# Scan products of a four-layer image kernel summed by TensorE transposes, tokens on partitions, in place of products with the identity

## The chip, the cores and the metric

The kernel runs on one core of a Trainium2 chip. The metric is device time in microseconds (us), the median of several runs. One core has five engines[...]: PE (TensorE, matrix products; its weight loads are listed apart as PEld), DVE (VectorE), ACT (ScalarE), POOL (GpSimd) and SP (SyncE, which here issues most DMA transfers).

## The reference, cut to what matters

Four layers run over four images of 384 channels and 48 x 48 points, each added to its own input. Layer 0, where the change lies, is a Mamba block over the 2,304 points of an image as a sequence (768 inner channels, 16 states):

```python
def step(h_prev, inp):
    x_t, dt_t, B_t, C_t = inp
    dA = jnp.exp(dt_t[..., None] * A)
    dBx = dt_t[..., None] * B_t[:, None, :] * x_t[..., None]
    h_new = dA * h_prev + dBx
    y_t = jnp.einsum('bds,bs->bd', h_new, C_t)
    return (h_new, y_t)
...
y = ys.transpose(1, 0, 2) + xin * D
y = y * jax.nn.silu(z)
out = y @ out_proj_w.T
```

So for each channel, 16 state sequences are scanned, each is multiplied with its C, the 16 products are summed, and D times the block's input is added (the skip). Then come a gate with silu(z), an output projection and a layer norm. Layers 1 to 3 (a block-wise Fourier filter with a gate, a depthwise 11 x 11 convolution, four experts chosen by token) do not change.

## The kernel before, in words

**Tiles and stages.** All data are float32. An image's sequence is cut into five chunks of 460 (the last 464) tokens. Channels lie on the 128 partitions and tokens along the free dimension, so 768 inner channels are six groups m, taken in three pairs p. A chunk has 96 units (`unit`, L615): for each pair, 16 states s with the two groups of the pair in turn. In a unit:

- SP loads bc, the rows B and C of state s repeated over all partitions (L622, once for two units);
- ACT makes da = exp(dt x A) in PSUM (L626; two buffers);
- POOL makes bu = u x B (L630; three buffers);
- DVE runs the scan (L634), into da, or for every third unit into g;
- the product with C goes into a tile g (six buffers): by DVE (L640), or for each third unit, whose scan wrote g itself, by POOL (L651);
- ACT copies the last scan value into `carry` for the next chunk (L642, L650);
- PE adds g into y, one PSUM bank for each group of the pair (tags y0 and y1, one buffer each), by a matrix product with the identity as stationary operand (`summed`, L590, the matmul at L600).

A product of POOL is put off: `late` holds it until two further units have issued their sums, and `after` keeps the two in that order on PE.

**Skip, gate and tail.** `skip` (L609) adds D x input in the middle of a pair, as a matmul with d_diag, a diagonal matrix made from D at the start (L296). `gate` (L655) multiplies y with silu(z) on DVE, straight from PSUM into zs. `tail` (L716) yields the output projection in four parts (`out_proj`, L661), the layer norm and three `residual` pieces, whose results are turned back to channels by transposes (L704).

**Order of the work.** `scans` (L414) runs over the 20 chunks. For each, `plan` lays pieces at unit numbers of the coming 96: projections of the next chunk (`project`, `project_z`, `expand`), `steps` (dt and u of a pair), gates and the tail of the chunk before. After each unit, `tile_layers` may also issue pieces of layers 1 to 3 of earlier images from a queue; the pace is by unit number. The queue starts with unit 24 of image 1 and is longer for images 2 and 3, which have experts too. From the pieces, the Tile scheduler makes the final order on each engine, so a piece may move by some places. After the last scan, the rest of layers 1 to 3 runs alone.

**PSUM.** A pool named mm has two banks for projections and other short results (tag mm), two for da and one each for y0 and y1; the background queue has its own.

## Time and profile before

| What | Value |
|---|---|
| median of 3 runs | 5762.97 us (5753.89 to 5764.69) |
| profiled execution: its own time | 5767.51 us |
| its span, first to last instruction | 5765.7 us |
| granted TensorE clock, mean | 0.953 |
| scan L634, one | 1.17 us |
| product on DVE L640 / on POOL L651, one | 0.63 / 1.16 us |
| da on ACT L626 / carry L642, one | 0.65 / 0.16 us |
| y matmuls L600 (g with ident) | 3,840, 0.60 us each as drawn |
| PE's idle time before y matmuls, ended by DVE's g L640 | 282 us |

Busy time is that in which an engine had an instruction in flight. Successive matmuls overlap in the pipeline, so the length drawn for one is more than it takes in a row of them; the distance from start to start shows that. The profiled execution lies 4.5 us over the median. The span is 1.8 us under its execution's own time.

### The profile page before, as it was taken

How to read it: one execution, taken by the hardware profiler on the slowest of the kernel's cores; microseconds unless marked ns; L12 is line 12 of the kernel's file. 1: busy time of each engine (PE TensorE's matmuls, PEld its weight loads, DVE VectorE, ACT ScalarE, POOL GpSimd, SP SyncE). 2: the span in 40 equal slices, each digit the busy share in tenths (PEclk: the TensorE clock that was granted, in tenths of full speed). 3: DMA queues.
4: the chain of work that ended last, by engine and by line, in shares of the span. 5: the costliest groups of instructions: out<-in, count | busy, mean ns of one | idle time of the engine just before them, and what ended most of it. 6: DMA issues, size and time to landing. Idle time of an engine off the chain costs nothing. (4 is left out here: it accounts for less than half of the span.)

```text
span 5765.7 us, 69035 instructions
## 1 busy us (share of the span) xinstructions
PE 5255.3 (91%) x23236; PEld 3320.9 (58%) x23236; DVE 4030.3 (70%) x5653; ACT 2956.1 (51%) x6424; POOL 3110.3 (54%) x2795
## 2 busy tenths in 40 slices
PE   6888888988889999999887999999988799999999
PEld 3333333433455546777433664877634375789999
DVE  5988988899997796666899577656698856451110
ACT  3555555555566654444655565444455564335321
POOL 3877888766586685555565366545465646000000
PEclk9999989988999999999998899999989899899999
DMA  4444444434344363233333235323332323311100
GB/s 135 134 137 135 143 127 139 124 118 121 118 139 137 114 206 108 89 106 112 112 119 106 90 120 171 99 88 102 103 112 95 121 93 125 114 45 43 54 23 26
DMA packets 396011, 634.19 MB, mean 110 GB/s; under 512 B 32373, under 2 KB 386789, under 8 KB 392190
## 3 DMA queue, kind: packets, MB, share of 16 engines
q1 hardware_dynamic: 382148, 618.58, 33.7%
q10 hardware_dynamic: 13498, 11.11, 0.7%
q8 instruction: 184, 3.01, 0.2%
q14 instruction: 181, 1.48, 0.1%
HBM read 571.80 MB, written 57.80 MB: 109 GB/s over the span
## 5 line engine op out<-in xcount | busy, mean ns | idle before, releaser
L630 POOL TENSOR_TENSOR bu<-u,bc 128x460 f32<-128x460 f32 (+1 forms) x1920 | 2217.2, 1167 | 1346.3 <-DVE g L634 632.8
L600 PE MATMUL y<-g,ident 128*128 128x460 f32 (+1 forms) x3840 | 1838.3, 597 | 286.8 <-DVE g L640 282.2
L626 ACT ACTIVATE da<-dt,a_neg 128x460 f32<-128x460 f32 (+1 forms) x1920 | 1232.1, 646 | 268.5 <-DVE g L640 166.2
L634 DVE TENSOR_TENSOR_SCAN da<-da,carry,bu 128x460 f32<-128x460 f32 (+1 forms) x1008 | 1165.7, 1170 | 196.6 <-ACT da L626 170.1
L600 PEld LDWEIGHTS y<-g,ident 128*128 128x128 f32 x3840 | 704.3, 201 | 1008.1 <-DVE g L640 541.7
L651 POOL TENSOR_TENSOR g<-g,bc 128x460 f32<-128x460 f32 (+1 forms) x660 | 766.7, 1162 | 249.4 <-DVE g L634 128.0
L640 DVE TENSOR_TENSOR g<-da,bc 128x460 f32<-128x460 f32 (+1 forms) x1260 | 775.9, 627 | 109.7 <-PE y L600 80.1
L634 DVE TENSOR_TENSOR_SCAN g<-da,carry,bu 128x460 f32<-128x460 f32 (+1 forms) x528 | 617.2, 1169 | 134.1 <-PE y L600 67.9
L1139 PEld LDWEIGHTS ph<-xe,w 128*128 128x128 f32 x4608 | 596.7, 191 | 54.3 <-issue 40.4
L1157 PEld LDWEIGHTS pout<-hr,w 128*128 128x128 f32 x4608 | 591.4, 190 | 54.7 <-issue 43.8
L1139 PE MATMUL ph<-xe,w 128*128 128x144 f32 x4608 | 620.1, 288 | 0.0
L1157 PE MATMUL pout<-hr,w 128*128 128x144 f32 x4608 | 616.4, 287 | 1.5 <-DVE xe L1168 1.5
L642 ACT COPY carry<-da 128x1 f32<-128x1 f32 x1008 | 158.0, 157 | 884.2 <-DVE g L640 882.5
L998 PEld LDWEIGHTS pc<-band,row 128*128 128x128 f32 x3456 | 455.8, 194 | 81.1 <-issue 48.6
L1147 ACT ACTIVATE hr<-ph,nb 128x144 f32<-128x144 f32 x768 | 235.5, 377 | 507.3 <-PE ph L1139 506.9
L998 PE MATMUL pc<-band,row 128*128 128x162 f32 (+14 forms) x3456 | 469.2, 286 | 6.5 <-ACT row L987 4.7
L669 PE MATMUL po<-w_out,zs 128*115 128x384 f32 (+1 forms) x960 | 346.6, 494 | 11.1 <-DVE zs L659 7.7
L878 DVE SCALAR_TENSOR_TENSOR dw<-pad,w_dw,dw 128x384 f32<-128x384 f32 x576 | 342.2, 609 | 14.4 <-ACT pad L866 11.2
L634 DVE TENSOR_TENSOR_SCAN da<-da,nil,bu 128x460 f32<-128x460 f32 x252 | 291.5, 1170 | 74.3 <-ACT da L626 66.4
L490 PE MATMUL pin<-xch,w_inx 128*128 128x463 f32 (+2 forms) x720 | 323.1, 579 | 10.8 <-DVE dt L585 4.7
L518 PE MATMUL pinz<-xch,w_inz 128*128 128x460 f32 (+1 forms) x720 | 306.0, 559 | 12.0 <-DVE xc L507 7.9
L507 DVE SCALAR_TENSOR_TENSOR xc<-pin,conv_w,xc 128x460 f32<-128x460 f32 (+1 forms) x360 | 246.9, 686 | 76.6 <-ACT xc L502 73.9
(170 smaller groups left out, 4754.8 us busy)
## 6 DMA issues: line engine op xcount, KB each, us to landing
bc<-bcd SPq DMA_DIRECT2D x768, 460.0 KB, 3.6
bc<-bcd SPq DMA_DIRECT2D x192, 464.0 KB, 3.6
xs<-x1d SPq DMA_DIRECT2D x24, 576.0 KB, 4.3
x2d<-xs SPq DMA_DIRECT2D x24, 576.0 KB, 2.9
x<-x2d SPq DMA_DIRECT2D x12, 1152.0 KB, 6.5
x3d<-x SPq DMA_DIRECT2D x12, 1152.0 KB, 5.9
xg<-x3d SPq DMA_DIRECT2D x24, 576.0 KB, 4.6
xe<-x3d SPq DMA_DIRECT2D x64, 216.0 KB, 2.6
```

The source lines that it names most:

```text
L490: nc.tensor.matmul(ps[:, lo : halo + n], lhsT=w_inx[:, k, bass.ts(j, P)], rhs=c["x"][:, k, lo : halo + n], start=k == 0, stop=k == CT - 1,)
L600: return nc.tensor.matmul(c["y", m][:, :n], lhsT=lhsT, rhs=src, start=c["terms", m] == 1, stop=c["terms", m] == DS + 1, skip_group_check=True,
L626: nc.scalar.activation(da[:, :n], c["dt", p][:, m % 2, :n], AF.Exp, scale=a_neg[:, m, s : s + 1])
L630: nc.gpsimd.tensor_mul(bu[:, :n], c["u", p][:, m % 2, :n], bc[:, 0, :n])
L634: nc.vector.tensor_tensor_scan(here[:, :n], da[:, :n], bu[:, :n], last if t else nil[:, 0:1], ALU.mult, ALU.add,)
L640: nc.vector.tensor_mul(g[:, :n], here[:, :n], bc[:, 1, :n])
L651: nc.gpsimd.tensor_mul(g[:, :n], here[:, :n], bc[:, 1, :n])
L669: nc.tensor.matmul(ps[:w, :C], lhsT=c["zs"][:, m, bass.ts(k, w)], rhs=w_out0[:, m, :], start=m == 0, stop=m == MT - 1,)
L878: nc.vector.scalar_tensor_tensor(v, src, w_dw[:, ct, k : k + 1], v, ALU.mult, ALU.add)
L998: nc.tensor.matmul(d["acc2"][:, : BANDS[k] * W].rearrange("p (h w) -> p h w", w=W)[:, lo - edges[k] : hi - edges[k], xlo:xhi], lhsT=d["row ...
L1139: nc.tensor.matmul(ps[:, bass.ts(m, EB)], lhsT=d["w1"][:, e, k, bass.ts(m, P)], rhs=d["x", s][:, k, :], start=k == 0, stop=k == CT - 1,)
L1157: nc.tensor.matmul(d["o"][:, bass.ts(m, EB)], lhsT=d["w2"][:, e, k, bass.ts(m, P)], rhs=d["h", s, e][:, k, :], start=e == 0 and m == 0 and ...
```

## The change

The sum of the 16 products and the skip is now made in another layout, with tokens on partitions. `turned` transposes a tile of [128 channels, n tokens] in four quarters of w = n/4 tokens (115 or 116), each into its own 128 columns of one bank; the four quarters accumulate over the units. D x input is made by ACT into a tile dx (from the buffers of g) and transposed as the first term at the start of the pair. When a pair has ended, `collect` copies both banks to SBUF tiles yt, and `gate` turns them back by four transposes into a bank of tag mm before DVE's multiplication. Gates stand three and six units into the next pair (or head the tail, at units 2 and 4 of the next chunk), the tail's other pieces one unit later or more. POOL's product is still added behind the sums of two later units, and on the side of DVE the copy of the carry still follows the product.

```diff
-        d_diag = wp.tile([P, MT, P], F32, name="d_diag")
-        for m in range(MT):
-            nc.scalar.activation(d_diag[:, m, :], ident, AF.Copy, scale=d_col[:, m : m + 1])
...
-            def summed(i, m, lhsT, src):
+            def turned(y, src, n, start, stop):
+                w = n // TT
+                return [
+                    nc.tensor.matmul(
+                        y[:w, bass.ts(k, P)],
+                        lhsT=src[:, bass.ts(k, w)],
+                        rhs=ident,
+                        is_transpose=True,
+                        start=start and k == 0,
+                        stop=stop,
+                        skip_group_check=True,
+                    )
+                    for k in range(TT)
+                ]
...
             def skip(i, p):
-                for m in (2 * p, 2 * p + 1):
-                    summed(i, m, d_diag[:, m, :], c["xc"][:, m, : CHUNKS[t]])
+                for h in range(2):
+                    m = 2 * p + h
+                    y = c["y", m] = mm.tile(
+                        [P, 512], F32, name=f"y{b}_{t}_{m}", tag=f"y{h}", bufs=1
+                    )
+                    dx = wk.tile([P, TM], F32, name=f"dx{b}_{t}_{m}", tag="g", bufs=6)
+                    nc.scalar.activation(
+                        dx[:, :n], c["xc"][:, m, :n], AF.Copy, scale=d_col[:, m : m + 1]
+                    )
+                    turned(y, dx, n, True, False)
...
-                    ins = summed(i, m, ident, g[:, :n])
-                    c["since"] = c.get("since", 0) + 1
-                    if late and (c["since"] >= 2 or (m % 2 and s == DS - 1)):
-                        after(late.pop(0)(), ins)
+                    ins = turned(c["y", m], g, n, False, s == DS - 1)
+                    c["since"] += 1
+                    if late and (c["since"] == 2 or (m % 2 and s == DS - 1)):
+                        for one in late.pop()():
+                            after(one, ins[-1])
...
+            def collect(i, p):
+                w = CHUNKS[t] // TT
+                for h in range(2):
+                    m = 2 * p + h
+                    yt = c["yt", m] = wk.tile([P, 512], F32, name=f"yt{b}_{t}_{m}", tag="yt")
+                    nc.scalar.copy(yt[:w, :], c["y", m][:w, :])

             def gate(i, m):
+                w = n // TT
+                ps = bank(f"pyb{b}_{t}_{m}")
+                for k in range(TT):
+                    nc.tensor.transpose(
+                        ps[:, bass.ts(k, w)], c["yt", m][:w, bass.ts(k, P)], ident[:w, :w]
+                    )
                 zm = c["zs"][:, m, :n]
-                nc.vector.tensor_tensor(zm, c["y", m][:, :n], zm, ALU.mult)
+                nc.vector.tensor_tensor(zm, ps[:, :n], zm, ALU.mult)
...
             def tail(i):
+                yield lambda: gate(i, MT - 2)
+                yield lambda: gate(i, MT - 1)
...
                 if i:
-                    for m in (MT - 2, MT - 1):
-                        plan(0, lambda m=m: gate(i - 1, m))
                     for k, piece in enumerate(tail(i - 1)):
-                        plan(3 + 2 * k, piece)
+                        plan(2 + 2 * k, piece)
...
-                            plan(2 * DS * p, lambda m=2 * p - 2 + h: gate(i, m))
+                            plan(2 * DS * p + 3 + 3 * h, lambda m=2 * p - 2 + h: gate(i, m))
...
-                    plan(2 * DS * p + DS, lambda p=p: skip(i, p))
                 for p in range(MT // 2):
+                    skip(i, p)
                     for q in range(2 * DS):
                         unit(i, 2 * p + q % 2, q // 2)
                         ...
+                    collect(i, p)
```

More of the change, by code (lines that the diff above doesn't have):

```diff
@@ L588, in steps, with skip @@
                     nc.gpsimd.tensor_mul(u[:, h, :n], dt[:, h, :n], c["xc"][:, 2 * p + h, :n])
-            def summed(i, m, lhsT, src):
+            def turned(y, src, n, start, stop):
[12 more added lines that the diff above has]
+                ]
+            def skip(i, p):
                 (b, t), c = G[i], st[i]
                 n = CHUNKS[t]
-                if ("y", m) not in c:
-                    c["y", m] = mm.tile(
-                        [P, 512], F32, name=f"y{b}_{t}_{m}", tag=f"y{m % 2}", bufs=1
-                    )
-                    c["terms", m] = 0
-                c["terms", m] += 1
-                return nc.tensor.matmul(
-                    c["y", m][:, :n],
-                    lhsT=lhsT,
-                    rhs=src,
-                    start=c["terms", m] == 1,
-                    stop=c["terms", m] == DS + 1,
-                    skip_group_check=True,
-                )
-            def skip(i, p):
-                (b, t), c = G[i], st[i]
-                for m in (2 * p, 2 * p + 1):
-                    summed(i, m, d_diag[:, m, :], c["xc"][:, m, : CHUNKS[t]])
+                for h in range(2):
+                    m = 2 * p + h
+                    y = c["y", m] = mm.tile(
+                        [P, 512], F32, name=f"y{b}_{t}_{m}", tag=f"y{h}", bufs=1
+                    )
+                    dx = wk.tile([P, TM], F32, name=f"dx{b}_{t}_{m}", tag="g", bufs=6)
[3 more added lines that the diff above has]
+                    turned(y, dx, n, True, False)
             def unit(i, m, s):
@@ L651, in unit @@
                     nc.gpsimd.tensor_mul(g[:, :n], here[:, :n], bc[:, 1, :n])
-                    late.append(lambda: summed(i, m, ident, g[:, :n]))
+                    late.append(lambda: turned(c["y", m], g, n, False, s == DS - 1))
                     c["since"] = 0
+            def collect(i, p):
+                (b, t), c = G[i], st[i]
+                w = CHUNKS[t] // TT
[3 more added lines that the diff above has]
+                    nc.scalar.copy(yt[:w, :], c["y", m][:w, :])
             def gate(i, m):
@@ L775, in scans @@
                         yield b, t, 2 * DS * p + q
+                    collect(i, p)
                 assert not todo
-            for m in (MT - 2, MT - 1):
-                gate(len(G) - 1, m)
             for piece in tail(len(G) - 1):
```

## The prediction

> **What bounds the kernel now.** I read the page first, for its shares of busy time.

> ```profile
> PE 5255.3 (91%) x23236; PEld 3320.9 (58%) x23236; DVE 4030.3 (70%) x5653; ACT 2956.1 (51%) x6424; POOL 3110.3 (54%) x2795
> ...
> PE   6888888988889999999887999999988799999999
> ...
> DVE  5988988899997796666899577656698856451110
> ...
> PEclk9999989988999999999998899999989899899999
> ```

> PE and DVE take turns: where one row is high, the other is often lower. So I cut the span at the chunks. Each of the 20 chunks (image b, chunk t; written b.t) has 96 scans, and every 96th scan start gives 96, 1026 (1.0), 1709 (1.3), 2126 (2.0), 2683 (2.2), 3239 (2.4), 3507 (3.0), 4076 (3.2), 4620 (3.4) and 4863 us (end of the scans). Busy time by stretch: columns are stretch, length, then PE, PEld, DVE, ACT, POOL, granted clock, DMA.

> ```profile
> 96.00:1026.00 930.00, 768.60 (x1814) 329.40 (x1813) 827.78 (x1030) 503.45 (x1065) 769.00 (x685) 0.94 0.42 135
> ...
> 2126.00:2683.00 557.00, 554.40 (x2970) 408.74 (x2969) 358.15 (x468) 268.07 (x659) 312.02 (x276) 0.98 0.37 114
> 2683.00:3239.00 556.00, 473.38 (x1440) 237.18 (x1439) 459.34 (x678) 297.19 (x621) 312.54 (x285) 0.90 0.36 112
> 3239.00:3507.00 268.00, 261.87 (x1366) 181.60 (x1365) 186.96 (x246) 169.98 (x322) 155.82 (x138) 0.99 0.34 114
> 3507.00:4076.00 569.00, 565.84 (x3011) 411.78 (x3010) 356.26 (x464) 271.05 (x663) 311.08 (x275) 0.99 0.36 110
> ...
> 4620.00:4863.00 243.00, 236.07 (x1294) 168.41 (x1292) 174.54 (x223) 158.72 (x307) 153.15 (x135) 0.99 0.35 116
> ```

> In image 0 DVE is busy 828 of 930 us (89%). In 2.0, 2.1, 2.4, 3.0, 3.1 and 3.4 it is busy only 63 to 72%, and PE is always in work. A busy PE need not be a full one, so I take start-to-start times from the timeline of PE (start, length, group; the length runs to the modelled end of the last one).

> ```profile
> 311.41 0.56 PE L704 MATMUL pt<-ident,on 115*128 115x115 f32 x4
> 311.81 0.95 PE L600 MATMUL y<-g,ident 128*128 128x460 f32 x2
> 312.59 1.71 PE L600 MATMUL y<-xc,d_diag 128*128 128x460 f32 x4
> 314.14 0.94 PE L600 MATMUL y<-g,ident 128*128 128x460 f32 x2
> ```

> Each start follows the last by 0.385 us for 460 columns ((314.14-312.59)/4) and by 0.10 us for a transpose of 115 columns ((311.81-311.41)/4): both 0.84 ns a column. The two differ in count: y has 3,840 matmuls for 1,920 units, two for each float32 product, while the transposes of L704 number 240 = 20 chunks x 3 x 4, one each. Pricing every matmul of the trace at 0.84 ns a column, or 0.11 us if that is more, fills 99% of 2.1 and 3.1, 92 to 94% of 2.0, 2.4, 3.0 and 3.4, and about 71% of image 0. Waits in 2.0 and 2.1 agree that DVE is starved from PE's side there:

> ```profile
> DVE da L634 <- ACT da L626: 72.9, 70, 4.8
> ACT hr L1147 <- PE ph L1139: 47.9, 35, 10.6
> ...
> DVE g L634 <- PE y L600: 34.5, 21, 6.6
> DVE g L640 <- PE y L600: 26.2, 17, 4.1
> ```

> ACT stands in its queue behind a PE result, and its late da holds up the scan; or g's six buffers are full because PE has not read them.

> [...] (columns: length, PE busy, clock):

> ```profile
> 302.24:305.65 3.41, 0.95 (x3) 1.00 0.00 0
> 305.65:309.07 3.42, 3.32 (x5) 0.50 0.28 90
> ```

> Three transposes in one window, half clock in the next, and the y products then 0.77 us apart instead of 0.385. Setting the column time of each window against the next clock, I find the border at about 0.38 of a window (a matmul with few input rows, such as L574 with 25, counts in proportion). Whether transposes count, the trace cannot say: no window has more than 0.11 of them, and none falls between the two readings. [...]

> **The change, part by part.**
> (a) A unit's sum: two matmuls of 460 columns, 0.77 us, become four transposes whose moving operand is ident, 128 columns: 4 x 128 x 0.84 = 0.43 us. Saved 0.34 us of PE. Weight loads pass from ident to slices of g, but L600's loads already waited for DVE in the trace, and a 128-column load sustains 0.11 us a matmul (L979: 0.108), so loads bind by at most 4 x 0.11 = 0.44. That accumulating transposes keep this rate no trace shows; bounds: 0.10 (115 columns) to 0.14 us each (a whole weight load of L704, not overlapped), so 0.40 to 0.56 a unit. I take 0.43.
> (b) skip: likewise 0.34 us saved 120 times. With (a), 102 x 0.34 = 35 us a chunk.
> (c) gate: 24 new transposes a chunk at 0.10 = 2.4 us of PE. Net 32 us a chunk, 650 us of PE work in all.
> (d) ACT gains six dx (0.65 us, as da of L626) and six copies of y (0.70 us, as L707, 460 columns): 8 us a chunk on an engine at 51 to 74%. Hidden under DVE or PE, except at (f). Six d_diag activations of 0.39 us go from the set-up, in DMA waits: nothing.
> (e) DVE's gate reads PSUM as before (0.63 us), 3 and 6 units later; behind it only out_proj waits, now from the sixth unit on. zs is rewritten from unit 15, after out_proj's last at 12 instead of 9: cover shrinks from six units to three, some 6 us. Nothing. SP's loads shift by a few places, no DMA is added.
> (f) At each end of a pair, ACT's copies of y wait for the last Pool product, and da of later units stands behind them. By the built order, from the end of the 31st scan: Pool one bu (1.17) then that product (1.17), 2.4; four transposes and their latency (0.26), 3.2; two copies, 4.6; carry and da, 5.5. DVE has before it a scan, product, scan, scan, product: 3 x 1.17 + 2 x 0.63 = 4.8. So da is late by about 0.8 us, three times a chunk. In the 14 chunks not bound by PE: 34 us. Bounds: 0 if the scheduler's slack covers it, 1.7 us each (72 us) at half clock.
> (g) Clock. With y at 0.43 us a unit of some 1.95 us, a window without other matmuls has 0.22 of work and goes cold even if transposes count. Re-pricing y in each window of the trace: cold windows of image 0 rise from 13 to 40%, of image 1 from 8 to 20%; of 2.1 and 3.1 stay at 1%. At half clock a unit's transposes take 0.86 us, still under the period, so little is late: 15 us (0 to 40).

> Sum. In the six PE-bound chunks PE gives up 32 us each, and DVE, at 174 to 187 us of busy time plus its usual 10% idle, has room to take most: 27 us x 6 = 162. In 1.3 and 1.4, PE at 0.9 and DVE at 0.83 to 0.86: 10 each, 20. Against this (f) 34 and (g) 15. Net 133 us off the profiled 5767.5 (span 5765.7 and 1.8 around it): 5634. That execution is 4.5 us over the median shown, so I say 5630. The stretch after 4863 us (903 us) has no y work and stays.

> **The rivals.**
> 1. Transposes do not count for the clock. Re-priced so, 67% of windows in image 0 and 57% in image 1 go cold, 23% in 2.0 and 3.0, 36% in 2.4 and 3.4. PE's load, its work over its clock, is then about today's 0.71 and 0.82 in images 0 and 1 (0.51/0.67 = 0.76, 0.61/0.71 = 0.85), and the gain shrinks: 15 us x 4 + 27 x 2 = 114, less 34 for (f) and 52 for cold projections that ACT and DVE wait for: 28. About 5735. [...] Against: bursts of three projections take 2.3 us and rewarm the clock.
> 2. Slower: the same, and PE becomes the bound in the thin chunks. Other matmuls of image 1 need 92 to 108 us a chunk, y and gate 46. Around 146 us of work in 222 us a chunk, PE fills at a mean clock of 0.66; that is the point. A saturated cold PE has 0.5 x 100/146 = 0.34 of counted work, under the border, so it can stay cold. At clock 0.55 image 1 takes 5 x (146/0.55 - 220) = 225 us more, 2.2 and 3.2 some 20 each: minus 114 plus 34 plus 265, about 5950; nearer the point, 5800. Central 5850.
> 3. The ACT wait of (f) takes the whole place of the removed work, at 2 to 3 us for 60 pair ends: 5765, no change.
> 4. Nothing of (f) and (g) shows, and DVE fills the PE-bound chunks entirely: 5560.

> **How the numbers follow.** Forecast 0.52, own range 5560 to 5690; rival 1 0.20 (5680 to 5790); 2 0.15 (5775 to 6000); 3 0.08; 4 0.05. The range 5560 to 5800 leaves out most of rival 2, half of 4 and the edges. A change within 0.2% can hardly be told from none here (the three runs spread by 0.19%). Faster: nearly all of the forecast and 4, two thirds of 1: 0.71. Same 0.06. Slower 0.23.

> **What would show it.** (a) L591, four starts 0.107 us apart in warm stretches. PE-bound gain: the scan starts of 2.1 and 3.1 about 270 us apart, not 299; image 0 within 2% of 930. (f) ACT's yt waits for PE near 1 us each. (g) the granted clock of image 0 near 0.8; if it is under 0.7, rival 1, and if image 1 is under 0.66 with PE full, rival 2. I am wrong if accumulating transposes run slower than 0.14 us each.

## The result, and the profile after

The changed kernel takes 5794.45 us (median of 4 runs, 5790.45 to 5797.41) against 5762.28 for the kernel before beside it: a ratio of 1.0058, interval 1.0041 to 1.0075. It is slower by 0.6%, where 5630 and "faster" were forecast. Its profiled execution took 5794.86 us, its span is 5793.0.

PE was relieved: it has 315 us less busy time, although it has 4,560 more matmuls. (The forecast's 650 us is priced at full clock and from start to start, so it is no forecast of busy time.) The page's first two parts, answering those of before:

```profile
PE 4940.3 (85%) x27796; PEld 3836.1 (66%) x27796; DVE 4034.3 (70%) x5653; ACT 3060.4 (53%) x6658; POOL 3111.3 (54%) x2795
...
PE   6677777778788888999877898999977798999999
...
DVE  5888888889988887667798668666788767451110
PEclk9677677888889988999878799899978789899999
```

PE's row is lower in most slices with scans, DVE's is no higher on the whole, and the clock of the first fifth, nearly all 9 before, is now mostly 6 and 7. Stretches cut at scan starts (columns: stretch, length, PE, PEld, DVE, ACT, POOL, clock, DMA) are image 0, then 2.0 with 2.1, 2.2 with 2.3, 2.4, 3.0 with 3.1, and 3.4:

```profile
95.00:1066.00 971.00, 716.14 (x2918) 501.34 (x2916) 835.25 (x1030) 531.27 (x1123) 769.63 (x685) 0.75 0.41 129
2201.00:2729.00 528.00, 505.66 (x3425) 440.88 (x3424) 353.04 (x466) 275.88 (x681) 312.27 (x276) 0.95 0.38 118
2729.00:3321.00 592.00, 468.48 (x2122) 319.68 (x2121) 468.43 (x691) 324.33 (x683) 312.47 (x285) 0.81 0.32 104
3321.00:3561.00 240.00, 216.82 (x1368) 170.93 (x1368) 182.34 (x238) 160.58 (x298) 155.63 (x138) 0.94 0.40 132
3561.00:4096.00 535.00, 514.01 (x3463) 443.13 (x3462) 348.68 (x458) 277.22 (x684) 311.63 (x276) 0.96 0.37 117
...
4664.00:4891.00 227.00, 204.89 (x1319) 171.09 (x1318) 168.82 (x216) 145.68 (x275) 150.03 (x133) 0.89 0.38 123
```

The two PE-bound stretches fell from 557 and 569 to 528 and 535 us. Image 0 rose from 930 to 971. 2.4 fell by 28, but 2.2 with 2.3 rose by 36. The next table, in us, cuts the whole difference at scan starts. Of the forecast, the 34 us of (f) are spread over its 14 chunks, and the 15 us of (g) stand in the row of image 0:

| stretch | before | after | difference | forecast |
|---|---|---|---|---|
| 2.0, 2.1, 3.0, 3.1 | 1125.2 | 1063.4 | -62 | -108 |
| 2.2 to 2.4, 3.2 to 3.4 | 1611.9 | 1626.8 | +15 | -44 |
| 1.3, 1.4 | 416.7 | 419.2 | +3 | -15 |
| image 0 and 1.0 to 1.2 | 1612.9 | 1687.4 | +75 | +34 |
| after the scans | 902.8 | 901.7 | -1 | 0 |

The price of a transpose was right. On the timeline of PE (start, length, group), first at half clock (0.50 granted from 601.5 to 609.5 us), last at full clock (1.00 from 2465 to 2467):

```profile
602.78 2.05 PE L591 MATMUL y<-ident,g 128*115 128x128 f32 x8 [0.62 <-DVE g L643]
606.53 2.91 PE L591 MATMUL y<-ident,g 128*115 128x128 f32 x12 [1.70 <-DVE g L643]
...
2465.74 1.04 PE L591 MATMUL y<-ident,g 128*115 128x128 f32 x8
```

At half clock, four more take 0.86 us more: 0.215 each. At full clock, starts are 0.109 us apart (median of all in the trace), where 0.107 was priced. What DVE and ACT wait for tells where the gain went (waits: total us, times, longest):

```profile
DVE da L637 <- ACT da L629: 331.3, 241, 13.2
...
ACT zs L522 <- PE pinz L515: 124.0, 68, 7.2
...
PEld y L591 <- ACT yt L665: 88.9, 34, 9.6
...
ACT dt L578 <- PE pdt L571: 65.9, 51, 3.8
```

In the kernel before, the first read 236.5, the second 83.1, the last 23.5, and the third did not exist. DVE's waits on y fell (those of its scans and products into g, together, from 170 to 95 us), but its waits on ACT's da rose by 95: in all, DVE's idle time in the part with scans is 998 us, before 973. So DVE waits for ACT where it had waited for PE. That alone doesn't make ACT the cost: in e10_skip_back (below), 86 us faster than the kernel before, DVE's wait on da still stands at 276.5.

At a pair end the wait for ACT can be read step by step (timeline, ACT and then DVE, at the end of the second pair of 0.2):

```profile
609.32 1.23 ACT L613 ACTIVATE dx<-xc,d_col 128x460 f32<-128x460 f32 x2
...
612.56 1.07 ACT L665 COPY yt<-y 115x512 f32<-115x512 f32 x2 [1.27 <-PE y L591]
613.51 0.20 ACT L654 COPY carry<-g 128x1 f32<-128x1 f32 x1
...
614.37 1.18 DVE L637 TENSOR_TENSOR_SCAN da<-da,carry,bu 128x460 f32<-128x460 f32 x1 [1.07 <-ACT carry L645]
```

A scan into g ended at 611.5; elsewhere in this stretch its carry and the next da follow at once, as at 608.64 and 608.74. Here they stand behind the two copies of y, which wait for PE's last transposes, and DVE, done with its product at 613.30, idles 1.07 us. Over the 60 pairs, DVE's idle time ahead of the first six scans of a pair, added up from the trace, rose from 193 to 245 us: 0.87 a pair. In the 14 chunks for which step (f) was meant it rose from 92 to 141, 49 us for the forecast's 34. Whether the copies are the cause of that is taken up below.

### The profile page after: what moved, and what is told of

It reads as the page before. It is cut to its first block, busy times and chain, and to the rows that moved or that the text cites. A ratio compares the mean times of both kernels' runs of the same rounds, so it can differ in the third digit from the quotient of the medians.

```text
span 5793.0 us, 78434 instructions
## 1 busy us (share of the span) xinstructions
PE 4940.3 (85%) x27796; PEld 3836.1 (66%) x27796; DVE 4034.3 (70%) x5653; ACT 3060.4 (53%) x6658; POOL 3111.3 (54%) x2795
## 5 line engine op out<-in xcount | busy, mean ns | idle before, releaser
L591 PE MATMUL y<-ident,g 128*115 128x128 f32 (+1 forms) x7680 | 1305.2, 318 | 403.0 <-DVE g L643 401.2
L591 PEld LDWEIGHTS y<-ident,g 128*115 128x115 f32 (+1 forms) x7680 | 1117.2, 202 | 700.1 <-DVE g L643 566.0
L1015 PE MATMUL pc<-band,row 128*128 128x162 f32 (+14 forms) x3456 | 493.6, 293 | 10.2 <-DVE x L1033 8.3
L1015 PEld LDWEIGHTS pc<-band,row 128*128 128x128 f32 x3456 | 466.7, 202 | 30.5 <-DVE x L1033 12.0
L515 PE MATMUL pinz<-xch,w_inz 128*128 128x460 f32 (+1 forms) x720 | 327.0, 588 | 33.9 <-DVE xch L730 12.6
L654 ACT COPY carry<-g 128x1 f32<-128x1 f32 x528 | 100.9, 191 | 392.8 <-DVE g L637 392.0
```

Source lines behind the costliest of these rows:

```text
L591: nc.tensor.matmul(y[:w, bass.ts(k, P)], lhsT=src[:, bass.ts(k, w)], rhs=ident, is_transpose=True, start=start and k == 0, stop=stop, skip ...
L1015: nc.tensor.matmul(d["acc2"][:, : BANDS[k] * W].rearrange("p (h w) -> p h w", w=W)[:, lo - edges[k] : hi - edges[k], xlo:xhi], lhsT=d["row ...
```

## Experiments

In the labels' numbers, 1 to 3 tell the clock from the order of the work, 4 and 8 undo the later tail, 5 to 7 put one side edit alone into the kernel before, and 9 to 12 follow from these. Ratios are to the kernel before on the same chip; differences between two of these kernels are taken from medians, and where the ratios say otherwise, that is said.

**e1_fill_thin: the clock given back.** Four more transposes, of a tile of zeros, go into y ahead of each unit's own in images 0 and 1 and in 2.2, 2.3, 3.2 and 3.3; the sums stay what they are.

```diff
+                        nc.tensor.matmul(
+                            y[:w, bass.ts(k, P)], lhsT=zero[:, :w], rhs=ident,
+                            is_transpose=True, start=False, stop=False,
...
+                    fill(i, c["y", m], n)
                     ins = turned(c["y", m], g, n, False, s == DS - 1)
```

> The changed kernel, with four more transposes a unit, of a tile of zeros, added into y in the chunks where PE has room (all of images 0 and 1; 2.2, 2.3, 3.2, 3.3). They change no sum; they only give TensorE work, 0.43 us a unit. Theory A (the half clock in windows with too little work costs the time, through projections that ACT waits for): the clock of image 0 rises from 0.75 to 0.93 or more, image 0 falls from 970 us to about 930, the 14 chunks give back most of the 136 us that they lost, total near 5660 us. Rival B (ACT's copies of y and dx, and what stands behind them, cost the time): image 0 stays near 970 us, total 5790 us or more.

5882.19 us, 1.0188 (1.0168 to 1.0207). Image 0 by stretches:

```profile
95.00:1076.00 981.00, 809.11 (x4823) 621.20 (x4821) 833.42 (x1031) 533.13 (x1124) 771.51 (x686) 0.94 0.41 128
```

With the clock back at 0.94, as before the change, image 0 is no shorter (980.5 against 971.9), and 2.2 and 2.3, back at 0.94 and 0.90, stay at 275 and 316 us. Giving the clock back doesn't shorten these stretches. But the filling itself costs PE time (65 of the 88 us by which this run is over the change lie in 1.3 and 1.4, where PE has other work), so this run alone doesn't price the clock. It shows one thing more: with nothing but transposes added, the clock of image 0 reads 0.94 in place of 0.75.

**e2_old_sum: everything but the transposes.** y is again a sum of products with ident, channels on partitions; D x by ACT, the copies of y and all places of gates and tail stay as in the change. The gate reads the copy, so the gate's transposes fall away.

```diff
                     nc.tensor.matmul(
-                        y[:w, bass.ts(k, P)],
-                        lhsT=src[:, bass.ts(k, w)],
-                        rhs=ident,
-                        is_transpose=True,
+                        y[:, :n],
+                        lhsT=ident,
+                        rhs=src[:, :n],
...
-                nc.vector.tensor_tensor(zm, ps[:, :n], zm, ALU.mult)
+                nc.vector.tensor_tensor(zm, c["yt", m][:, :n], zm, ALU.mult)
```

> The changed kernel with the old sum: y by products with ident, channels on partitions; dx, the copies of y by ACT, the places of gate and skip as in the change; the gate's transposes left out (DVE reads the copy). Theory A: the clock of image 0 is back at 0.93 or more, image 0 at 930 to 945 us, the six PE-bound chunks as slow as before, total 5765 to 5785 us. Rival B: the thin chunks are as slow as in the changed kernel and the PE-bound ones as slow as before, total near 5890 us.

5847.99 us, 1.0137 (1.0117 to 1.0157). Image 0:

```profile
95.00:1063.00 968.00, 789.20 (x1817) 336.40 (x1815) 846.27 (x1033) 530.97 (x1124) 775.00 (x686) 0.91 0.41 129
```

Without any transposed sum, at a clock of 0.91, image 0 takes 968 us, as in the change. So a loss of this size needs neither the transposes nor a low clock. But the run also brings in a cost that the change doesn't have: its gate reads both operands from SBUF, where that of the change reads one from PSUM. The gates of the change, then those of this run (count, shortest/median/longest in ns):

```profile
L677 DVE TENSOR_TENSOR zs<-pyb,zs x120: 610/628/644, 166.3 to 4899.3; 128x460 f32<-128x460 f32 x96, 128x464 f32<-128x464 f32 x24
...
L668 DVE TENSOR_TENSOR zs<-yt,zs x120: 610/642/1617, 164.5 to 4953.2; 128x460 f32<-128x460 f32 x96, 128x464 f32<-128x464 f32 x24
```

In this run 58 gates start while POOL is inside an instruction. Of these, 55 take 0.74 to 1.62 us and end 0.49 to 0.50 us after that instruction of POOL; none of the other 62 takes over 0.65. In the change 70 gates start so, and none is long. In all, the gates take 110 us here and 75 in the change. So of the 79 us lost here (0.0137 x 5770), up to 34 belong to this reading, and the 46 us (0.0079 x 5770) by which the change is faster than this run are not all the gain of its transposes.

**e3_both: both ways.** The new way only in chunks 0, 1 and 4 of images 2 and 3, the old one elsewhere.

```diff
+            def new(i):
+                b, t = G[i]
+                return b >= 2 and t in (0, 1, 4)
```

> Both ways in one kernel: the changed sum, skip and gate in 2.0, 2.1, 2.4, 3.0, 3.1 and 3.4, all of the kernel before in the other 14 chunks. Both theories: the six chunks keep what they won (105 us by the two traces), the others run as before: near 5660 us. Above 5700 us would mean that gains and losses are not of the chunks in which they show.

5687.20 us, 0.9851 (0.9831 to 0.9871). Images 0 and 1 are as before the change (930.9 and 1100.1); 2.0, 2.1, 3.0 and 3.1 fall by 75. But 2.4 takes 269.1 us (before 268.5) and 3.4 takes 235.8 (242.5): 0 and 7 us of the forecast's 27 each.

**e4_tail_back: the tail at its old units.** The last two gates stand at units 1 and 2, out_proj begins again at unit 3 and not at 6.

```diff
-                yield lambda: gate(i, MT - 2)
-                yield lambda: gate(i, MT - 1)
...
+                    for h in range(2):
+                        plan(1 + h, lambda m=MT - 2 + h: gate(i - 1, m))
-                        plan(2 + 2 * k, piece)
+                        plan(3 + 2 * k, piece)
```

> The changed kernel with the tail back in its old place: the last two gates at units 1 and 2 of the next chunk, out_proj from unit 3 (after the change: gates at 2 and 4, out_proj from 6). Theory C (the tail, three units later, runs into the next pair's steps and the projections, and ACT and DVE wait there): image 0 falls from 972 to about 940 us, total 5720 us or less. Rival B (ACT's copies and dx): image 0 stays within 6 us of 972, total 5780 to 5800 us. Rival A (clock): the same as B, since the clock stays at 0.75 in image 0.

5736.09 us, 0.9929 (0.9904 to 0.9954): 58 us under the change (74 by the ratios), for a shift of at most three units that step (e) had at nothing. It does not come where it was expected: image 0 falls by 7 us, not by 32. The four PE-bound chunks fall by 29 and 2.2 to 2.4 with 3.2 to 3.4 by 24. The chunks 2.0 with 2.1 now:

```profile
2203.00:2717.00 514.00, 497.49 (x3435) 431.29 (x3434) 354.09 (x469) 276.70 (x682) 311.57 (x276) 0.98 0.39 122
```

514 us, in place of 528. The four PE-bound chunks together are at 1034.7, 91 under before. The clock of image 0 stays at 0.75.

**e5_tail_late, e6_dx, e7_copies: one side edit alone in the kernel before.** The first moves the tail by three units:

```diff
-                        plan(3 + 2 * k, piece)
+                        plan(6 + 2 * k, piece)
```

> The kernel before with one edit: the tail's pieces (out_proj on) from unit 6 in place of 3; gates, skip and sum untouched. Theory C: image 0 rises from 930 to 955 us or more, total 5800 us or more. Rivals A and B: no change, within 10 us of the kernel before.

The second makes D x by ACT at the start of the pair, and sums it by a product with ident:

```diff
-                    summed(i, m, d_diag[:, m, :], c["xc"][:, m, : CHUNKS[t]])
+                    dx = wk.tile([P, TM], F32, name=f"dx{b}_{t}_{m}", tag="g", bufs=6)
+                    nc.scalar.activation(
+                        dx[:, :n], c["xc"][:, m, :n], AF.Copy, scale=d_col[:, m : m + 1]
+                    )
+                    summed(i, m, ident, dx[:, :n])
```

> The kernel before with one edit: the skip as in the change (D x by ACT at the head of each pair), added by a product with ident. Theory C: within 10 us of the kernel before. Rival B: its share of ACT's new work, 0.66 us for each of 120, plus what waits behind it: 15 to 40 us slower.

The third copies both banks by ACT at the pair's end; gates read the copies, three and six units into the next pair (the last two at units 1 and 2), and the tail stays:

```diff
+                    nc.scalar.copy(yt[:, :n], c["y", m][:, :n])
...
-                nc.vector.tensor_tensor(zm, c["y", m][:, :n], zm, ALU.mult)
+                nc.vector.tensor_tensor(zm, c["yt", m][:, :n], zm, ALU.mult)
...
-                            plan(2 * DS * p, lambda m=2 * p - 2 + h: gate(i, m))
+                            plan(2 * DS * p + 3 + 3 * h, lambda m=2 * p - 2 + h: gate(i, m))
```

> The kernel before with one edit: ACT copies each y to SBUF at the end of the pair, and DVE's gate reads the copy three and six units later (last pair: units 1 and 2 of the next chunk; the tail stays from unit 3). Theory C: within 15 us of the kernel before. Rival B: 2 to 3 us for each of 60 pair ends, in the DVE-bound chunks alone some 40 us in image 0, 80 us or more in all.

| edit alone | time | ratio (interval) | cost | where |
|---|---|---|---|---|
| tail later | 5802.65 | 1.0050 (1.0033 to 1.0066) | 29 us | 2.0, 2.1, 3.0, 3.1 +15, image 0 +9 |
| D x by ACT | 5795.33 | 1.0036 (1.0018 to 1.0053) | 21 us | 2.2 to 2.4, 3.2 to 3.4 +26 |
| copies, gates | 5816.22 | 1.0065 (1.0048 to 1.0082) | 38 us | image 1 +23, image 0 +11, 2.2 to 2.4, 3.2 to 3.4 +18 |

The costs are taken from the ratios. The third is not a price of the copies: its gates read both operands from SBUF too, 56 of the 64 that start inside an instruction of POOL are long, and together they take 107 us, 32 more than before. What is left for the copies and the later gates may be little. The first two costs, 50 us, and those longer gates would about make up e2_old_sum's 79.

For the tail, the trace of e5_tail_late shows how work is held up. In the kernel before, the layer norm stands at unit 11, clear of `steps`, which is planned at unit 16; in e5_tail_late it stands at 14. PE and then ACT in 0.2 of e5_tail_late, by the timeline:

```profile
500.76 1.00 PE L704 MATMUL pt<-ident,on 115*128 115x115 f32 x4 [4.80 <-DVE xc L507]
501.69 1.90 PE L574 MATMUL pdt<-xd,w_dt 25*128 25x460 f32 x2
503.51 3.43 PE L600 MATMUL y<-xc,d_diag 128*128 128x460 f32 x4
506.88 1.90 PE L574 MATMUL pdt<-xd,w_dt 25*128 25x460 f32 x2
...
508.81 0.55 ACT L581 ACTIVATE dt<-pdt 128x460 f32<-128x460 f32 x1 [4.64 <-PE pdt L574]
```

PE idles 4.80 us while the layer norm runs and is then at half its pace (four skip products take 3.43 us, and 1.71 at 312.59 of the kernel before, where the granted clock is 1.00), the second pdt comes behind them, and ACT waits 4.64 us for it with the da of later units in its queue. Over the whole run, ACT's wait for pdt is 63.9 us, before 23.5. Added up over the chunks, DVE's idle time moves from units 8 to 15 into 16 to 23, and in this run more comes out there than went in:

| DVE idle, us | units 8 to 15 | 16 to 23 | 24 to 39 | 0 to 39 |
|---|---|---|---|---|
| before | 218 | 64 | 293 | 618 |
| e5_tail_late | 122 | 207 | 277 | 640 |
| after | 50 | 177 | 334 | 621 |
| e4_tail_back | 148 | 80 | 276 | 568 |
| e10_skip_back (below) | 153 | 82 | 252 | 529 |

In the changed kernel the same shift shows, but units 8 to 23 together are as idle with the tail late (227 us) as with the tail back (229). The 53 us by which units 0 to 39 are less idle in e4_tail_back lie in units 24 to 39. So that the later tail costs time in the change is shown by undoing it; what holds up DVE in those units is not shown.

For D x by ACT the rows show where, not why: in 2.2 to 2.4 of e6_dx, 19 us longer than before, ACT is only 9 us busier and DVE 1. The edit does three things at once: it gives ACT work, it moves the skip from the middle of the pair to its start, and it takes two of the six buffers of g there. No run separates them.

```profile
2678.00:3521.00 843.00, 752.28 (x2803) 422.74 (x2803) 647.27 (x924) 476.10 (x959) 467.95 (x423) 0.90 0.35 111
```

**e8_both_tail: e3_both with the tail at its old units everywhere.**

```diff
-                        plan((2 if new(i - 1) else 3) + 2 * k, piece)
+                        plan(3 + 2 * k, piece)
```

> The earlier kernel with both ways, and the tail in its old place everywhere (in 2.0, 2.1, 2.4, 3.0, 3.1, 3.4 the new sum with the last gates at units 1 and 2; the kernel before in the other 14). Theory C (the moved tail cost the PE-bound chunks what they did not win): these six fall from 1555 us to about 1490, total 5630 to 5650 us. If the tail does not matter there: 5685 us.

5667.76 us, 0.9830 (0.9817 to 0.9843). 2.0, 2.1, 3.0 and 3.1 are 95 us under before. Chunk 2.4, whose other PE work is in place here:

```profile
3188.58:3450.51 261.93, 241.24 (x1570) 196.00 (x1569) 185.42 (x245) 174.08 (x328) 154.18 (x137) 0.93 0.36 120
```

PE's busy time fell by 21 us against before, the chunk by 7. Now PE waits 21 us in it (before 6), mostly for ACT's row (9) and DVE's g (8), and ACT's row still waits 30 us for PE's pr (before 33). So 2.4 had a PE that was full but not alone in setting the length. That the convolution's steps, which follow each other through three engines, are the other part is likely from these waits, and not shown.

**e9_half_fill and e12_skip_fill: the clock again.** Two transposes of zeros (not four) for a unit, in e9_half_fill added to e4_tail_back in image 0, 1.0 to 1.2, 2.2, 2.3, 3.2 and 3.3; in e12_skip_fill added to e10_skip_back in image 0 and 1.0 to 1.2. The sums stay what they are.

```diff
+                    for k in (0, 1):
+                        nc.tensor.matmul(
+                            y[:w, bass.ts(k, P)], lhsT=zero[:, :w], rhs=ident,
```

> The changed kernel with the tail back, and two transposes of a tile of zeros a unit, half as many as in the first filled kernel, in image 0, 1.0 to 1.2, 2.2, 2.3, 3.2 and 3.3 (0.22 us of PE a unit; no sum changes). Theory A (clock): the clock of image 0 rises from 0.75 to 0.85 or more, image 0 falls from 965 to 950 us or less and 2.2, 2.3, 3.2, 3.3 together from 1157 to 1130 or less, total near 5690. If the clock costs nothing there: both within 10 us, total 5730 to 5745.

> The earlier kernel with tail and skip in their old places (10), with two transposes of zeros a unit in image 0 and 1.0 to 1.2 (no sum changes). If the half clock costs what the last filled kernel showed (18 us in image 0): image 0 falls from 940 to 930 us or less at a clock of 0.88 or more, total 5665 to 5675. If not: 5684 or more.

e9_half_fill: 5718.33 us, 0.9916 (0.9901 to 0.9931), 18 under e4_tail_back (8 by the ratios), with image 0's clock at 0.88 (0.75) and image 0 at 947.6 (965.3). e12_skip_fill: 5694.69, 0.9872 (0.9855 to 0.9890), 10 over e10_skip_back (8 by the ratios), with the clock at 0.88 (0.79) and image 0 at 945.4 (939.6). One gains, the other loses, and each interval overlaps that of the kernel without the filling. Neither run shows a price of the clock beyond some 20 us, and its sign stays open: the extra transposes also take time on PE, 0.22 us a unit at the 0.109 us measured for one in the changed kernel, and may shift the order.

**e10_skip_back: D x on PE again.** e4_tail_back with the skip in the middle of the pair, four products of an input slice with d_diag, in the transposed layout; no dx.

```diff
+                    for k in range(TT):
+                        nc.tensor.matmul(
+                            c["y", m][:w, bass.ts(k, P)],
+                            lhsT=c["xc"][:, m, bass.ts(k, w)],
+                            rhs=d_diag[:, m, :],
...
+                    plan(2 * DS * p + DS, lambda p=p: skip(i, p))
...
-                    skip(i, p)
```

> The changed kernel with the tail back and with D x back on PE in mid-pair (the input turned by the diagonal matrix; no dx, ACT's 120 activations of 0.66 us gone, and no wait of the pair's first transposes for them; PE has 120 x 0.86 us of products in place of 120 x 0.43). If D x on ACT costs in the changed kernel what it cost alone (21 us, most of it in 2.2 and 3.2): total near 5715 us, these two at 255 to 265 us in place of 270. If the loss alone was one of order only: 5730 us or more.

5684.36 us, 0.9858 (0.9843 to 0.9873): 52 us under e4_tail_back (41 by the ratios), though PE has more work. Image 0 and 2.0 with 2.1:

```profile
94.00:1033.00 939.00, 691.77 (x3040) 486.65 (x3038) 827.39 (x1027) 517.58 (x1092) 768.66 (x685) 0.79 0.42 133
...
2145.00:2659.00 514.00, 501.53 (x3460) 438.20 (x3461) 356.53 (x470) 269.57 (x666) 310.93 (x275) 0.97 0.39 122
```

The gain over e4_tail_back is in images 0 and 1 (26 and 27 us), which now lie 9 and 13 us over before, image 0 with the clock still at 0.79. It is not in 2.2 and 3.2, where it was expected: they stay at 272 and 271. DVE's idle time ahead of the first six scans of a pair falls from 220 to 189 us. With both shifts undone, the four rows with scans of the first table read -91 (forecast -108), -15 (-44), -9 (-15) and +31 us (+34).

**e11_both_skip: the best found.** e10_skip_back, with sum, skip and gate of the kernel before in image 0 and 1.0 to 1.2.

```diff
+            def new(i):
+                b, t = G[i]
+                return b >= 2 or (b == 1 and t >= 3)
```

> The earlier kernel with tail and skip in their old places (10), with the sum, skip and gate of the kernel before in image 0 and 1.0 to 1.2. These eight chunks go back from 1644 to 1613 us, the rest stays: total 5650 to 5660 us, below all kernels so far.

5661.76 us, 0.9808 (0.9794 to 0.9822): faster than both kernels, by 1.9% and, through the two ratios, 2.5%. Image 0 is back at 930:

```profile
95.00:1025.00 930.00, 764.71 (x1814) 328.07 (x1812) 827.95 (x1031) 503.49 (x1065) 768.76 (x685) 0.94 0.43 135
```

## Why the prediction was wrong, by its own steps

**(a) to (c), the saving on PE: right.** Transposes at full clock start 0.109 us apart, priced at 0.107. The scan starts of 2.1 and 3.1, said to be about 270 us apart, are 270.8 and 271.1.

**The sum's "27 us x 6": right for four chunks, wrong for two.** With the tail back, 2.0, 2.1, 3.0 and 3.1 gained 91 to 96 us of the 108. 2.4 and 3.4 did not gain 27 each: in e8_both_tail, with their other work in place, 7 each. That 2.4 is 28 us shorter in the change itself is mostly work that left it. Counting matmuls other than those of y and of the gates, 2.3 has 723 in place of 475, 2.4 has 929 in place of 1,163; in 3.3 and 3.4 it is 640 for 438 and 889 for 1,081. Most of the difference is the convolution's (L1015), which the built order put earlier. 2.2 to 2.4 together went from 824.6 to 831.8. The step read each chunk alone, and took PE at 92 to 94% to mean that PE sets its length. The 20 us of 1.3 and 1.4 did not come either (+3 in the change, -9 in e10_skip_back).

**(d) "Hidden under DVE or PE, except at (f)": the first step that failed.** D x by ACT costs 21 us alone, and 41 to 52 in the changed kernel once the tail is back. ACT's share of busy time, 51 to 74%, was no cover. Part of the cost stands at the pair starts, where DVE's idle time falls by 31 us when D x leaves ACT. A likely way is that da, on which a scan waits, stands behind the new activations on ACT, as it stands behind the copies at 613.51 above; the skip's new place and the two buffers of g are rivals that no run tells apart.

**(e) "Nothing": the second.** The prediction checked zs, SP's loads and DVE's operand, but not what the tail now stands beside. In e5_tail_late the layer norm, three units later, runs into `steps`. Cost: 29 us alone, 58 to 74 in the change, there by a way that is only in part seen. Steps (d) and (e) together cost 110 us in the change (115 by the ratios).

**(f) 34 us, bounds 0 to 72: the wait is there, its size is not settled.** The step's own terms add up to some 0.5 us a pair end (5.24 less 4.77), not 0.8. DVE's idle time at pair starts rose by 52 us, near the forecast, but that is in good part luck: in e10_skip_back, where the copies stay and only D x and the tail are back, it is 189 us, before 193. In the step's 14 chunks it is then 106 us, 14 over before. Copies and later gates alone cost 38 us, up to 32 of them by gates that read SBUF. Copies could not be undone in the transposed layout, where a gate must read tokens back, so their price inside the change was not tried.

**(g) 15 us: not refuted.** The clock of image 0 fell to 0.75, further than "near 0.8", and image 0 is 4.5% over 930, not within 2%. But e10_skip_back takes 32 us off image 0 at a clock of 0.79, so most of the added length has another cause.

**The rivals.** 1, whose premise no trace showed, falls: in the trace of the change transposes count for the clock (below). The trace of before already spoke against it. That no window there falls between the two readings holds only without the convolution's 864 transposes (L979). With them a window has up to 0.31 of transposes, not 0.11, and three windows fall clearly between (at 1746, 3255 and 4613 us; the one at 3255 has work for 0.49 of its time with transposes, 0.30 without). Full clock follows each of the three, as it must if transposes count. 2, which ended on the right side, did so by luck: its point was a clock of image 1 under 0.66, and it is 0.87. 3, an ACT wait in the place of the removed work, is nearest in kind, but it named pair ends alone, and put 2 to 3 us where DVE idled 0.87 more. 4 falls.

Put right, the sum has (d) and (e) at some 110 us together, not at nothing, and 7 us each for 2.4 and 3.4, not 27. With tail and skip back, the change gains 86 us (82 by the ratio), where 133 were forecast. What is left open is the rest of the misfit, shifts of 15 to 30 us in single chunks that go with the built order, how the later tail costs twice as much in the change as alone, and why D x by ACT does too.

## What to carry to other kernels

An engine that is busy half of the time may still not take work for nothing (here ACT, busy 51% of the span, took D x for 21 us alone): look at what will stand behind the new instruction, and price that wait at every place. When a piece is moved by some units, lay it beside all that is planned at its new place, not only beside its own buffers. Read a saving over a group of stages: the built order carries work across their borders, and a full engine may be one of several that set a stage's length (in 2.4, 21 us less of busy PE went with a chunk 7 us shorter). And when a run puts one part of a change back to price it, look for what it brings in: here an operand that moved from PSUM to SBUF made up to 34 of 79 us.

## What the runs showed of the hardware

```profile
813.01:816.43 3.42, 2.75 (x13) 2.43 (x13) 2.26 (x3) 2.37 (x6) 3.42 (x4) 0.50 0.47 138
816.43:819.84 3.41, 3.41 (x19) 3.41 (x18) 3.32 (x5) 1.62 (x5) 2.56 (x3) 0.50 0.41 134
819.84:823.25 3.41, 2.73 (x16) 1.81 (x16) 3.41 (x6) 1.67 (x5) 3.41 (x4) 0.99 0.28 86
```

At 0.84 ns a column (0.385 us from start to start for 460 columns in the kernel before), the transposes of the first make 0.35 of a window and the clock stays at half (0.50); those of the second make 0.48, and the third runs at full clock (0.99). Of the 224 windows in this trace that hold transposes and no other matmul, all 161 that they fill to less than 0.35 are followed by half clock, and all 34 that they fill to 0.40 or more by full clock. The whole trace has some 1,700 windows, and one fits if full clock follows it when its work is over a border and half clock when it is under. (The work of a matmul is laid from 0.12 us after its start.) With the border at 0.375 of a window and each matmul weighted by its input rows over 128, 7 don't fit if transposes count in full; without that weight 70 don't (in the trace of before, at the same border, 7 and 32). If transposes count nothing, some 160 don't fit wherever the border is put. So what rival 1 assumed of transposes does not hold for these, in float32.

Transposes that accumulate ran at the rate of plain ones: 0.109 us from start to start for 128 columns at full clock, as those of L979 in the kernel before (0.109, the median), and 0.215 us at half clock. In image 0, a clock raised from 0.75 to 0.88 by filling went with 18 us less (e9_half_fill against e4_tail_back), and one raised from 0.79 to 0.88 with 6 us more (e12_skip_fill against e10_skip_back). And of the 58 gates of e2_old_sum, products of DVE with both operands in SBUF, that started inside an instruction of POOL, 55 took 0.74 to 1.62 us and ended 0.49 to 0.50 us after that instruction. Of the 70 such gates of the change, with one operand in PSUM, none took over 0.65 us.
